# Layer 0's softmax weights in four buffers instead of three, with one buffer less for the sums of key tiles, the denominator and the numerator

## The chip, the cores and the metric

The kernel runs on one core of a Trainium2 chip. The metric is the device time of the whole program in microseconds. The core has five engines that run side by side and meet through semaphores: TensorE (PE, whose weight loads are listed apart as PEld), VectorE (DVE), ScalarE (ACT), GpSimd (POOL) and SyncE (SP, which issues the DMAs here). Everything is computed in fp32.

## The reference

Two attention layers on an image `x` of 128 rows by 256 places by 256 channels, each with a group norm ahead of it and a residual around it. The change lies in the first one, layer 0, with 8 heads of 32 channels:

```python
def _L0_conv_ref(msa_repr, pair_repr, gate_proj, qkv_proj, out_proj, bias_proj):
    bias = jnp.einsum('nijz,zh->nhij', pair_repr, bias_proj)[:, None]
    gate = jax.nn.sigmoid(msa_repr @ gate_proj).reshape(bs, s, r, head, c)
    q, k, v = jnp.split(msa_repr @ qkv_proj, 3, axis=-1)
    ...
    sim = jnp.einsum('nsqhc,nskhc->nshqk', q, k) * scale
    sim = jax.nn.softmax(sim, axis=-1)
    sim = sim + bias
    attend = jnp.einsum('nshqk,nskhc->nsqhc', sim, v) * gate
    out = attend.reshape(bs, s, r, cm) @ out_proj
    return out

x = x + _L0_conv_ref(_gn(x), ...)     # layer 0
x = x + _L1_conv_ref(_gn(x), ...)     # layer 1: 4 heads of 64 channels, a band of 16 places
```

The softmax runs over 256 keys for each of 256 queries, separately in each of the 128 rows and 8 heads. Since the bias is added after the softmax, the kernel computes `((sum of e v) / z + (sum of bias v)) * gate`, where `e` are the exponentials and `z` their sum.

## The kernel before, in words

The program has three stretches. The first one loads `x` for the statistics and turns the pair bias into `bias_sb`. The second one, the loop of layer 0, takes the 128 image rows one by one. The third one does the same for layer 1. Layer 0 writes its rows to a buffer in DRAM, from which layer 1 reads.

In the loop of layer 0, channels or keys lie on the 128 partitions. The 256 keys make two key tiles (`kt`), and the 8 heads make two halves of four heads (`half`). For a row `s`, the functions do this:

- `scores(s, half)`: 8 products `sim` on PE (line 640), four heads side by side in strips of 32 partitions, into four PSUM banks, one for each head. Then four exponentials `ex` on ACT (line 651), one for each bank. A buffer of `ex` holds four heads by two key tiles by 256 queries, 8 KB in a partition, so a row fills two of them.
- `join_tiles(s, half, j)`: DVE adds the two key tiles of two heads into `both` (line 657), 4 KB in a partition, two instructions for a half.
- `sum_heads(s)`: PE multiplies `both` by ones, so that `zs` (line 681) is the softmax denominator, and multiplies the bias by `v`, which gives `bv` (line 667).
- `divide(s, zs)`: ACT copies `zs` to `z` (line 694). DVE makes the denominator `d` with the gate (line 696) and its reciprocal (line 697).
- `attend(s)`: PE multiplies `ex` by `v`, which gives `av` (line 667, 32 records for a row, the first half of the heads before the second). DVE makes the numerator `t` as `bv * z + av` (lines 712 and 713) and `at` as `t * d` (line 715).
- `stretch(names, i)`: the projections of the pair of rows `i`, `q` and `k` in one step of the loop, `v` and `g` (the gate) in the next, with PE and ACT taking turns: `f.take("15")` and its like are copies on ACT (lines 621 to 627), and `p2qk` or `p2vg` collect one product of each.
- `by_channel(out_sb, ...)` gives `po` on PE (line 513), and `finish` adds the residual on DVE (line 723).

The loop works one row behind itself: step `s` computes the scores of row `s` and finishes row `s - 1`. The order on PE, ACT and DVE is the order in which the program text issues the instructions (`manual_schedule`); only POOL's instructions are placed by a scheduler. One step issues:

```python
scores(s, 0); zs = sum_heads(s - 1); join_tiles(s, 0, 0); divide(s - 1, zs)
# in even steps: ACT makes the exponential of g (line 786)
scores(s, 1); attend(s - 1)
join_tiles for (0, 2), (1, 0), (1, 2); least(s - 1, z)
stretch(...); normal(s + 4); finish(s - 1, by_channel(out_sb, ...))
```

The score tiles and the projections share a ring of five PSUM banks, taken in turn; a step takes 12 tiles from it (8 scores, 3 in `stretch`, 1 for `po`). `av`, `bv` and `zs` have one bank each.

Each tile tag of a pool has a number of buffers (`bufs`), used in turn. The pool `att0` holds `ex`, `both`, `z`, `d` and `t`, with two buffers for each tag that doesn't say otherwise. Before, `ex` and `both` have three. The first instruction that writes a buffer anew waits until the last reader of its former content has ended. With three buffers of `ex`, the second half of row `s` takes the buffer of the first half of row `s - 1`, which `attend(s - 1)` reads. With three buffers of `both`, the first half of row `s` takes that of the second half of row `s - 2`.

Of the kernel before, what the change touches and what calls it, by code (L numbers as in the profile page):

```python
# [9 lines left out]
F32 = mybir.dt.float32  # L10
# [5 lines left out]
P = 128  # L16
R = 256
# [22 lines left out]
def conv_preact_kernel(  # L40
# [38 lines left out]
    def sim_bank(name):  # L79
        return bank("sim", name)  # L80
# [45 lines left out]
    for part, first in ((seen[:, 0], 0), (seen_high, -KB)):  # L126
        nc.gpsimd.memset(part, 1.0)
        for b in range(NB):
            d = first + KB * b - QLO[b]
# [409 lines left out]
    with ExitStack() as both:  # L539
# [11 lines left out]
        with ExitStack() as lay0:  # L551
            row = lay0.enter_context(tc.tile_pool(name="row0", bufs=2))
            att = lay0.enter_context(tc.tile_pool(name="att0", bufs=2))
# [79 lines left out]
            def scores(s, half):  # L633
                i, r = divmod(s, 2)
                q, k = res["q", i], res["k", i]
                sims = [sim_bank(f"sim{s}_{half}_{j}") for j in range(4)]
                for kt in range(2):
                    for j in range(4):
                        p0 = D0 * j
                        nc.tensor.matmul(  # L640
                            sims[j][:, kt, :],
                            lhsT=k[p0 : p0 + D0, 2 * r + half, kt * P : (kt + 1) * P],
                            rhs=q[p0 : p0 + D0, 2 * r + half, :],
                            start=True, stop=True,
                        )
                ex = att.tile([P, 4, 2, R], F32, tag="ex", name=f"ex{s}_{half}", bufs=3)
                both = att.tile([P, 4, R], F32, tag="both", name=f"both{s}_{half}", bufs=3)
                hd[s, half] = (ex, both)

                for j in range(4):  # L650
                    nc.scalar.activation(ex[:, j], sims[j], AF.Exp, scale=1.0 / math.sqrt(D0))  # L651
# [7 lines left out]
            def products(to, s, weights):  # L659

                i, r = divmod(s, 2)
                v = res["v", i]
                for half in range(2):
                    for kt in range(2):
                        for j in range(4):
                            c0 = kt * P + j * D0
                            nc.tensor.matmul(  # L667
                                to[D0 * j : D0 * (j + 1), half, :],
                                lhsT=v[:, 2 * r + half, c0 : c0 + D0], rhs=weights(4 * half + j, kt),
                                start=(kt == 0), stop=(kt == 1),  # L670
                            )
# [17 lines left out]
            def divide(s, zs):  # L689
                if s < 0:  # L690
                    return
                i, r = divmod(s, 2)
                z = att.tile([P, 2, R], F32, tag="z", name=f"z{s}")
                nc.scalar.activation(z, zs, AF.Identity, accum_out=zsum[:, s : s + 1])
                d = att.tile([P, 2, R], F32, tag="d", name=f"d{s}")
                nc.vector.scalar_tensor_tensor(d, res["g", i][:, 2 * r : 2 * r + 2, :], 1.0, z, op0=ALU.add, op1=ALU.mult)
                nc.vector.reciprocal(d, d)  # L697
                hd[s, "z"] = (z, d)
# [5 lines left out]
            def attend(s):  # L704
                if s < 0:
                    return
                (ex0, _), (ex1, _), bv0 = hd.pop((s, 0)), hd.pop((s, 1)), hd.pop(s)
                av = ps_av.tile([P, 2, R], F32, tag="av", name=f"av{s}")
                products(av, s, lambda h, kt: (ex0, ex1)[h // 4][:, h % 4, kt, :])
                z, d = hd.pop((s, "z"))  # L710
                t = att.tile([P, 2, R], F32, tag="t", name=f"t{s}")
                nc.vector.tensor_tensor(t, bv0, z, ALU.mult)
                nc.vector.tensor_tensor(t, av, t, ALU.add)
                at = row.tile([P, 2, R], F32, tag="at", name=f"at{s}")
                nc.vector.tensor_tensor(at, t, d, ALU.mult)  # L715
                st[s]["at"] = at
# [52 lines left out]
            with tc.manual_schedule(engines={mybir.EngineType.PE, mybir.EngineType.Activation, mybir.EngineType.DVE}):  # L769
# [8 lines left out]
                for s in range(S + 1):  # L778
                    if s < S:
                        scores(s, 0)  # L780
                    zs = sum_heads(s - 1)
                    join_tiles(s, 0, 0)
                    divide(s - 1, zs)
                    if s % 2 == 0 and s < S:
                        e = res["g", s // 2]
                        nc.scalar.activation(e, e, AF.Exp, scale=-1.0)
                    if s < S:
                        scores(s, 1)
                    z = hd[s - 1, "z"][0] if s > 0 else None
                    attend(s - 1)  # L790
                    for half, j in ((0, 2), (1, 0), (1, 2)):
                        join_tiles(s, half, j)
                    least(s - 1, z)
                    if s == S - 1:
                        most1 = join_most(st1, stats1, 1)
                        load1(0)
                        load1(1)
                    stretch(("qk", "vg")[s % 2], s // 2 + 1)
                    normal(s + 4)
                    if s % 2 == 1:  # L800
                        sum_rows((s + 3) // 2)
                    if s > 0:
                        finish(s - 1, by_channel(out_sb, 0, st[s - 1]["at"], f"po{s - 1}"))
# [6 lines left out]
        with ExitStack() as lay:  # L810
            ps_av = psum(lay, "1", 4, 0)
            row = lay.enter_context(tc.tile_pool(name="row1", bufs=4))
            att = lay.enter_context(tc.tile_pool(name="att1", bufs=2))
# [146 lines left out]
            for s in range(0, S + 4, 2):  # L960
                pair = lambda first: (first, first + 1)
                if s < S:
                    for r in pair(s):
                        scores(r)
                if s <= S:
                    for r in pair(s - 2):
                        attend(r)
                for r in pair(s - 4):
                    project(r)
                for r in pair(s + 2):  # L970
                    for n in (1, 2):
                        piece(r, n)
                for r in pair(s + 2):
                    piece(r, 3)
                for r in pair(s + 4):
                    piece(r, 0)
                for r in pair(s - 4):
                    finish(r)
                if s <= S:
                    for r in pair(s - 2):  # L980
                        divide(r)
# [195 lines left out]
```

## Time and profile before

| what | value |
|---|---|
| time, median of 3 runs (lowest to highest) | 3416.61 us (3416.49 to 3417.72) |
| profiled execution: time, span of its instructions | 3416.59 us, 3414.9 us |
| PE busy | 3303.8 us, 97% |
| DVE, ACT, POOL busy | 2560.7, 1768.3, 1139.6 us |
| loop of layer 0, about 337 to 2245 us | 1908 us, PE busy 1864 us |
| one step of that loop, mean of two | 15.77 us |
| reciprocal of `d`, one | 3353 ns |
| exponential `ex`, one | 603 ns |
| mean granted TensorE clock | 0.988 |

The profile is of one execution. Busy time is the time in which an engine had an instruction under way; the profiler models the ends of matmuls, so a busy PE can still have slack in the distance between the starts of two matmuls. The steps of layer 0 come in two kinds: with `q` and `k` in their `stretch`, and with `v` and `g`. A row's products on PE come as merged pieces in the timeline: `x32` is 32 matmul records in one piece.

### The profile page before, as it was taken

What the parts mean: (1) busy time and instruction counts of PE and PEld (TensorE: products, weight loads), DVE (VectorE), ACT (ScalarE), POOL (GpSimd) and SP (SyncE); (2) the same over time, 40 slices, a digit from 0 to 9 for tenths busy, and PEclk for the clock granted to TensorE, in tenths of its full rate; (3) what the DMA queues carried; (4) which work ended last, traced back from release to release, by engine and by line L of the source; (5) the groups of instructions that cost most, each with busy time, mean ns of one, the idle gap of its engine ahead of it and who ended that gap; (6) DMA issues with size and microseconds to landing.
All of it is one profiled execution on the core that took longest, in us unless ns stands there. A gap on an engine that the chain in (4) does not pass through costs nothing.

```text
span 3414.9 us, 86753 instructions
## 1 busy us (share of the span) xinstructions
PE 3303.8 (97%) x37193; PEld 2488.6 (73%) x37193; DVE 2560.7 (75%) x3794; ACT 1768.3 (52%) x3866; POOL 1139.6 (33%) x1135
## 2 busy tenths in 40 slices
PE   6899999999999999999999999989999999999997
PEld 4566666666666666666666666678888888888886
DVE  4747877777787787777778777757777777777776
ACT  4565555555555555555555555534444444444442
POOL 3033333333333333333333333223333333333332
PEclk8999999999999999999999999999999999999999
DMA  9922111111111111111111111002222222222221
GB/s 380 409 58 57 44 36 35 35 35 32 38 32 32 38 32 38 32 38 32 32 38 32 37 33 32 20 20 64 53 62 63 64 61 54 63 64 63 55 60 45
DMA packets 346328, 209.37 MB, mean 61 GB/s; under 512 B 273608, under 2 KB 339152, under 8 KB 339664
## 3 DMA queue, kind: packets, MB, share of 16 engines
q1 hardware_dynamic: 345040, 201.37, 20.4%
q8 instruction: 295, 4.83, 0.6%
q0 software_dynamic: 752, 2.36, 0.2%
q14 instruction: 97, 0.79, 0.1%
q10 hardware_dynamic: 144, 0.00, 0.0%
HBM read 136.59 MB, written 67.11 MB: 60 GB/s over the span
## 4 chain that ended last, share of the span: by engine, by line
PE 87%; ACT 5%; DMA 3%; DVE 3%; issue 1%; SPq 0%; ACTq 0%; POOL 0%; DVEq 0%
PE sim L640 8%; PE p1v L841 7%; PE av L667 7%; PE 1po L513 7%; PE p1q L513 7%; PE po L513 7%; PE p1k L513 6%; PE bv L667 6%; PE pv L614 6%; PE pq L610 5%; PE pk L610 4%; PE zs L681 4%; DMA xs<-in_x_dram 3%; PE pg L610 3%; PE 1sim L862 3%; PE 1avz L894 2%
## 5 line engine op out<-in xcount | busy, mean ns | idle before, releaser
L651 ACT ACTIVATE ex<-sim 128x512 f32<-128x512 f32 x1024 | 528.6, 603 | 500.4 <-PE sim L640 274.8
L919 DVE RECIPROCAL 1rz<-1z 128x512 f32<-128x512 f32 x128 | 427.9, 3343 | 174.2 <-ACT 1z L917 174.2
L872 POOL TENSOR_TENSOR 1p<-1ex,seen 128x768 f32<-128x768 f32 x128 | 233.8, 1826 | 735.9 <-ACT 1ex L870 735.9
L657 DVE TENSOR_TENSOR both<-ex 128x512 f32<-128x512 f32 x512 | 340.9, 707 | 125.0 <-ACT ex L651 124.9
L697 DVE RECIPROCAL d<-d 128x512 f32<-128x512 f32 x128 | 429.2, 3353 | 4.4
L640 PE MATMUL sim<-q,k 32*128 32x256 f32 x4096 | 295.9, 401 | 1.1 <-ACT ex L651 1.1
L630 POOL TENSOR_TENSOR v<-v,twovg 128x256 f32<-128x256 f32 x64 | 46.5, 726 | 736.1 <-ACT twovg L756 736.1
L833 ACT ACTIVATE 1q<-p1q,bqk 128x256 f32<-128x256 f32 x256 | 107.3, 470 | 345.0 <-PE p1q L513 345.0
L640 PEld LDWEIGHTS sim<-q,k 32*128 32x128 f32 x4096 | 187.0, 184 | 102.3 <-issue 88.0
L513 PE MATMUL po<-at,out_sb 128*128 128x256 f32 x1024 | 247.2, 385 | 11.8 <-DVE at L715 11.8
L667 PE MATMUL av<-ex,v 128*32 128x256 f32 x4096 | 247.5, 382 | 0.0
L513 PE MATMUL 1po<-1at,w_out_t 128*128 128x256 f32 x1024 | 242.0, 390 | 5.0 <-DVE 1at L921 5.0
L513 PE MATMUL p1q<-xn,w_in_t 128*128 128x256 f32 x1024 | 243.8, 381 | 2.0 <-DVE xn L493 1.1
L667 PE MATMUL bv<-bias_sb,v 128*32 128x256 f32 x4096 | 244.5, 379 | 0.0
L513 PE MATMUL p1k<-xn,w_in_t 128*128 128x256 f32 x1024 | 241.9, 379 | 0.0
L841 PE MATMUL p1v<-w_in_t,xn 128*64 128x128 f32 x4096 | 237.9, 274 | 0.0
L841 PEld LDWEIGHTS p1v<-w_in_t,xn 128*64 128x64 f32 x4096 | 222.3, 137 | 21.5 <-issue 21.5
L513 PEld LDWEIGHTS 1po<-1at,w_out_t 128*128 128x128 f32 x1024 | 191.3, 192 | 54.8 <-ACT 1z L917 23.9
L723 DVE TENSOR_TENSOR o<-po,xt 128x512 f32<-128x512 f32 x128 | 88.6, 692 | 190.0 <-PE po L513 190.0
L513 PEld LDWEIGHTS po<-at,out_sb 128*128 128x128 f32 x1024 | 197.8, 194 | 40.4 <-issue 7.7
L630 POOL TENSOR_TENSOR q<-q,twoqk 128x256 f32<-128x256 f32 x64 | 46.5, 727 | 529.3 <-ACT twoqk L756 529.3
L513 PEld LDWEIGHTS p1q<-xn,w_in_t 128*128 128x128 f32 x1024 | 195.6, 191 | 29.2 <-issue 1.3
(226 smaller groups left out, 6748.1 us busy)
## 6 DMA issues: line engine op xcount, KB each, us to landing
pr<-in_L_conv_pair_repr_dram SPq DMA_DIRECT2D x32, 1024.0 KB, 23.3
x<-o SPq DMA_DIRECT2D x64, 512.0 KB, 2.8
yg<-x SPq DMA_DIRECT2D x64, 512.0 KB, 4.3
out_dram<-1o SPq DMA_DIRECT2D x256, 128.0 KB, 4.1
xg<-in_x_dram SPq DMA_DIRECT2D x252, 128.0 KB, 3.2
xs<-in_x_dram SPq DMA_DIRECT2D x15, 2048.0 KB, 21.7
xs<-in_x_dram SPq DMA_DIRECT2D x2, 1024.0 KB, 17.9
qkv_sb<-in_L_conv_qkv_proj_dram POOLq DMA_DIRECT2D x4, 192.0 KB, 13.4
```

The lines of the kernel that those rows point to most:

```text
L513: nc.tensor.matmul(ps[:, m, :], lhsT=w[:, kt, col + m * P : col + (m + 1) * P], rhs=xn[:, kt, :], start=(kt == 0), stop=(kt == 1),)
L610: nc.tensor.matmul(out, lhsT=stationary(self.w, n), rhs=moving, start=first, **flags)
L614: nc.tensor.matmul(out[:, cols], lhsT=moving[:, cols], rhs=stationary(self.w, n), start=first and t2 == 0, **flags)
L640: nc.tensor.matmul(sims[j][:, kt, :], lhsT=k[p0 : p0 + D0, 2 * r + half, kt * P : (kt + 1) * P], rhs=q[p0 : p0 + D0, 2 * r + half, :], sta ...
L651: nc.scalar.activation(ex[:, j], sims[j], AF.Exp, scale=1.0 / math.sqrt(D0))
L657: nc.vector.tensor_tensor(both[:, j : j + 2], ex[:, j : j + 2, 0, :], ex[:, j : j + 2, 1, :], ALU.add)
L667: nc.tensor.matmul(to[D0 * j : D0 * (j + 1), half, :], lhsT=v[:, 2 * r + half, c0 : c0 + D0], rhs=weights(4 * half + j, kt), start=(kt == ...
L681: nc.tensor.matmul(zs[D0 * j : D0 * (j + 1), half, :], lhsT=ones[:, 0:D0], rhs=both[:, j, :], start=True, stop=True,)
L697: nc.vector.reciprocal(d, d)
L841: nc.tensor.matmul(ps[KB * half : KB * (half + 1), b, :], lhsT=xn[:, kt, KB * b : KB * (b + 1)], rhs=w_in_t[:, kt, 2 * C + P * half : 2 * ...
L872: nc.gpsimd.tensor_tensor(p.rearrange("p j (r c) -> p (j r) c", c=WROW)[:, :, 0 : 2 * WSTEP] .rearrange("p r (t c) -> p r t c", c=WSTEP)[: ...
L919: nc.vector.reciprocal(rz, z)
```

## The change

`ex` gets a fourth buffer. Each half of row `s` then takes the buffer of the same half of row `s - 2`, which `attend(s - 2)` read in the step before. `both` goes from three buffers to two, so the first half of row `s` takes that of the first half of row `s - 1`, which the `zs` products of the same step read. `d` and `t` go from two buffers to one. In a partition, `ex` takes 8 KB more, `both` 4 KB less, `d` and `t` 2 KB less each, so the pool's size stays as it was. The order of the instructions on every engine stays as it was too; what differs is which semaphores some of them wait for.

```diff
-                ex = att.tile([P, 4, 2, R], F32, tag="ex", name=f"ex{s}_{half}", bufs=3)
-                both = att.tile([P, 4, R], F32, tag="both", name=f"both{s}_{half}", bufs=3)
+                ex = att.tile([P, 4, 2, R], F32, tag="ex", name=f"ex{s}_{half}", bufs=4)
+                both = att.tile([P, 4, R], F32, tag="both", name=f"both{s}_{half}")
...
-                d = att.tile([P, 2, R], F32, tag="d", name=f"d{s}")
+                d = att.tile([P, 2, R], F32, tag="d", name=f"d{s}", bufs=1)
...
-                t = att.tile([P, 2, R], F32, tag="t", name=f"t{s}")
+                t = att.tile([P, 2, R], F32, tag="t", name=f"t{s}", bufs=1)
```

In the built programs these waits differ, step by step: the first exponential of a second half no longer waits for DVE, and its wait for PE now means its own score tile; each of the other three gets a wait for its own tile, which the first one's later wait had covered. The first `both` of a row gets a wait for PE. The first product of `p2qk` or `p2vg` loses a wait for PE and keeps that for ACT. The copy of `g` gets a wait for DVE.

## The prediction

> **What bounds the kernel now.** I read the page first. PE (TensorE) is busy for 97% of the span and holds 87% of the chain that ended last; ACT holds 5%, DVE 3%. The loop of layer 0, where all four edits lie, runs from about 337 to 2245 us: 1908 us, with PE busy 1864 us. The page also shows what the fourth buffer aims at: the exponentials have 500 us of idle time before them.
>
> ```profile
> PE 3303.8 (97%) x37193; PEld 2488.6 (73%) x37193; DVE 2560.7 (75%) x3794; ACT 1768.3 (52%) x3866; POOL 1139.6 (33%) x1135
> PE 87%; ACT 5%; DMA 3%; DVE 3%; issue 1%; SPq 0%; ACTq 0%; POOL 0%; DVEq 0%
> L651 ACT ACTIVATE ex<-sim 128x512 f32<-128x512 f32 x1024 | 528.6, 603 | 500.4 <-PE sim L640 274.8
> ```
>
> Idle time on ACT costs only what PE later waits for. So I asked next who waits for whom, PE and its weight loads (PEld) alone, from 400 to 2150 us (111 rows of 15.77 us). A line gives engine, line, releaser, total us, times, longest.
>
> ```profile
> PE pq L610 <- ACT midq L625: 8.8, 56, 0.2
> PE pv L614 <- ACT midv L623: 0.4, 1, 0.4
> ...
> PEld sim L640 <- issue: 77.5, 210, 0.4
> ...
> PEld pq L610 <- ACT ex L651: 23.1, 56, 0.4
> PEld pv L614 <- ACT ex L651: 22.6, 55, 0.4
> ```
>
> PE waits for ACT's small copies, never for `ex`. Two rows of PEld do name `ex`, 45.7 us in all: either a real stall or only a neighbour in time. Last, the timeline of one row from 1313 us: ACT alone, DVE alone, and the PE pieces between. Columns: start, duration, engine, line, operation; in brackets the idle time before it and what ended it.
>
> ```profile
> 1315.34 2.06 ACT L651 ACTIVATE ex<-sim 128x512 f32<-128x512 f32 x4 [2.14 <-PE sim L640]
> ...
> 1317.83 1.09 ACT L786 ACTIVATE g<-g 128x1024 f32<-128x1024 f32 x1
> 1320.19 2.06 ACT L651 ACTIVATE ex<-sim 128x512 f32<-128x512 f32 x4 [1.27 <-PE av L667]
> 1322.11 0.62 ACT L621 COPY q<-pq 128x512 f32<-128x512 f32 x1
> 1322.95 0.59 ACT L621 COPY k<-pk 128x512 f32<-128x512 f32 x1 [0.21 <-PE pk L610]
> ```
>
> ```profile
> 1315.25 1.07 PE L681 MATMUL zs<-both,ones 128*32 128x256 f32 x16
> ...
> 1317.97 0.74 PEld L640 LDWEIGHTS sim<-q,k 32*128 32x128 f32 x16 [0.41 <-issue]
> ...
> 1319.05 1.93 PE L667 MATMUL av<-ex,v 128*32 128x256 f32 x32
> ...
> 1320.91 0.30 PEld L610 LDWEIGHTS pq<-xn,qkv_sb 128*128 128x128 f32 x2 [0.41 <-ACT ex L651]
> ```
>
> ```profile
> 1316.45 0.69 DVE L657 TENSOR_TENSOR both<-ex 128x512 f32<-128x512 f32 x1 [1.48 <-ACT ex L651]
> 1318.07 0.90 DVE L696 SCALAR_TENSOR_TENSOR d<-g,z 128x512 f32<-128x512 f32 x1 [0.93 <-ACT z L694]
> ...
> 1323.73 0.69 DVE L715 TENSOR_TENSOR at<-t,d 128x512 f32<-128x512 f32 x1
> 1324.34 1.89 DVE L657 TENSOR_TENSOR both<-ex 128x512 f32<-128x512 f32 x3
> ```
>
> The wait is plain: the second half's exponentials start at 1320.19, 1.27 us after ACT went idle, because their buffer is still read by the first half of `av`. The trap is the 0.41 us before `pq`. The switch from `bv` to `sim` at 1317.97 has the same 0.41 and no ACT in it. In the records, start of the last `av` matmul to start of the first `pq` or `pv` is 309 ns in all 111 rows; `bv` to `sim` is 309 ns in all 111, `po` to `sim` too. A switch that is equally long where ACT plays no part isn't waiting for ACT.
>
> **What the Trainium skill says.** "TensorEngine Tiling (Array Packing)", Key Properties: changing the tiling mode drains TensorE. The trace agrees: PEld pauses 0.33 to 0.41 us wherever the tile shape changes (`sim` 32*128, `zs` 128*32, `pq` 128*128), and not between `zs` and `bv`, which share one. "Perfetto Trace Analysis", Optimization Strategy: the same gap repeated on the engine that should be saturated can mean too few buffers. Here the repeated gap is on ACT, 52% busy, so the sentence doesn't make it worth time. Same page, Identifying Dependency Chains: an instruction waiting on several engines may get an EventSemaphore ahead of it. The trace has them: 222 on ACT at L651 in those 111 rows, and on PE at 51 ns each.
>
> **The change part by part.**
>
> *ex, three to four buffers.* Removed: the wait of the second half's exponentials for `av`. They can start once their `sim` is there. The first half shows the lag: `sim` at 1314.17, `ex` at 1315.34, so 1.17 us. The second half's `sim` starts at 1317.97, so `ex` at about 1319.14 instead of 1320.19: 1.05 us earlier (ACT is free at 1318.92, after the exponential of `g`). The other kind of row, with `pv` and `pg`, goes from 1304.40 to 1302.14 + 1.17 = 1303.31: 1.09 us. Over 127 rows ACT gains some 136 us of lead. Who uses it? (a) PE needs the banks that the exponentials free. The five banks go round, 12 tiles a row: `pq` takes the bank of the first half's last score tile, `pk` that of `ex` number 1 of the second half (free at 1320.79, used at 1321.88), `p2qk` that of number 2 (free near 1321.27, used at 1322.75). None is late. (b) The next copy on ACT, `q` at 1322.11, has its product at 1322.05, so it can come 0.01 us earlier; `v` in the other row is 0.04 us late at most. PE writes that bank again at 1323.61, 0.88 us after the copy ends. From the `k` copy on, ACT waits for PE, so the lead is gone. (c) DVE adds the second half's key tiles at 1324.34, behind `at`, when `ex` has been done for 2 us. Path: 0. From below, were all 309 - 216 = 93 ns of that switch a wait: 127 x 93 ns = 11.8 us gained. I take 0.
>
> *both, three to two.* Added: the first key-tile sum of a row waits for the `zs` products of the row before. All 16 end at 1316.32 and the sum starts at 1316.45, held by `ex`; the eight it needs end 0.4 us sooner. Behind it on DVE stands `d`, with 0.93 us of idle time, then the reciprocal, `t`, `at`, for which `po` waits. To cost anything the sum must slip over 0.93 us. 0, and nothing from above: its releaser has ended before the wait begins. A gain has no way in.
>
> *d and t, two to one.* Writer and last reader are both DVE, in order: `at` of one row (to 1324.42) comes before the next row's `d` (some 10 us on). 0; what hides it is DVE's own other work.
>
> *Small waits.* The `p2` product loses its second wait, the first sum gains one, `g`'s copy gains one on DVE. At PE's 51 ns an extra semaphore instruction is worth 127 x 51 ns = 6.5 us if bare. But `p2qk` follows the product before it after 216 ns, a plain slot; DVE idles 0.16 to 1.48 us before the sum; ACT idles 0.20 us before `g`'s copy. I take 0, from -6.5 to +6.5 us. No DMA and no work on SP or POOL moves.
>
> *Neighbours.* The exponentials now run beside all of `av`, not its last half. In the records groups of four `av` matmuls start 216 ns apart before and after `ex` starts, and `bv` runs beside the first half's exponentials at the same 216. 0.
>
> Sum: 0 against the profiled execution (3414.9 us of span, 3416.59 in all), which stands 0.02 us under the median of 3416.61. What remains is the clock: the pauses at the end of layer 0 are followed by stretches of 3.4 us at a granted 0.50 in the windows view, and one such stretch more or less is 1.7 us of work. Two either way make 3.4.
>
> **The rivals.** *Faster.* ACT's lead is used after all: the row "PEld pq <- ACT ex" is a real wait. For: the profile names it. Against: the twin switch of 309 ns. Price: 11.8 us, so 3404.8 us. Chance 0.05.
>
> *Slower.* Exponentials beside the first half of `av` slow its matmuls, since ACT writes one `ex` buffer while PE streams another. Place: the first four of eight groups; price: per ns and group 4 x 127 = 0.5 us. It decides (over 0.2%, 6.8 us) from 13 ns a group, 6%. At 10% of 216 ns it is 11 us: 3427.6 us. For: this overlap is new for those groups. Against: the last four groups already run so, at 216 ns. "PSUM — Partial Sum Buffer", PSUM bank collisions, says that a clash in a bank raises an error, not a stall; no run here shows it. Chance 0.07.
>
> *It doesn't do what it says.* Something else holds the exponentials, such as `g`'s, which ends just 0.2 us before they could start. Then nothing moves: same time, inside the likeliest case.
>
> **How the numbers follow.** No change: 0.88, at 3416.6 us. A measurement of this kernel tells about 0.2% from no change, 6.8 us. Within 3.5 us either way comes the clock's spread; I widen to 3412.6 and 3420.6 for about half of the bare semaphore bound. That leaves out both rivals, 0.12, and a little of the main case.
>
> **What would show it.** Right: the row "ACT ex <- PE av" is gone, the second half's `ex` starts about 1.05 us sooner against `sim`, new idle time of about 1 us stands before the copies of `q` and `v`, the PEld switch into `pq` is still 0.41 us, and `zs`, `d` and `po` keep their distances, the row its 15.77 us. Wrong: a switch into `pq` below 309 ns (faster), or `av` groups over 216 ns or `d` later against `zs` (slower).

## The result, and the profile after

The changed kernel takes 3417.65 us (median of 4 runs, 3411.70 to 3418.18) beside 3416.94 us for the kernel before (4 runs): a ratio of 0.9998 over all these runs, not of the two medians, with a 95% interval of 0.9981 to 1.0015. The forecast of no change, at 3416.6 us, holds.

The wait that the fourth buffer was to remove is gone all the same. This is the page's group of exponentials in the profile after; its last columns are the idle time before them and what ended most of it. The idle time was 500.4 us before.

```profile
L651 ACT ACTIVATE ex<-sim 128x512 f32<-128x512 f32 x1024 | 528.8, 603 | 362.9 <-PE sim L640 362.9
```

So 137.5 us of ACT's idle time left that place. Where did it go? This is the timeline of one row of the profile after, ACT alone, from 1310 us on. It answers to the ACT lines of the prediction.

```profile
1310.95 2.07 ACT L651 ACTIVATE ex<-sim 128x512 f32<-128x512 f32 x4 [2.14 <-PE sim L640]
...
1313.45 1.09 ACT L786 ACTIVATE g<-g 128x1024 f32<-128x1024 f32 x1
1314.75 2.07 ACT L651 ACTIVATE ex<-sim 128x512 f32<-128x512 f32 x4 [0.22 <-PE sim L640]
1317.70 0.59 ACT L621 COPY q<-pq 128x512 f32<-128x512 f32 x1 [0.88 <-PE pq L610]
1318.56 0.59 ACT L621 COPY k<-pk 128x512 f32<-128x512 f32 x1 [0.28 <-PE pk L610]
```

The second half's exponentials now wait 0.22 us instead of 1.27, and for their own scores. The copy of `q`, which had no idle time before it, now has 0.88 us, released by PE. ACT moved its pause from ahead of the exponentials to behind them. The same row on the other engines, taken from timelines of the profile after:

```profile
1310.86 1.07 PE L681 MATMUL zs<-both,ones 128*32 128x256 f32 x16
...
1313.59 0.74 PEld L640 LDWEIGHTS sim<-q,k 32*128 32x128 f32 x16 [0.41 <-issue]
...
1314.67 1.93 PE L667 MATMUL av<-ex,v 128*32 128x256 f32 x32
...
1316.53 0.30 PEld L610 LDWEIGHTS pq<-xn,qkv_sb 128*128 128x128 f32 x2 [0.41 <-ACT ex L651]
```

```profile
1312.07 0.69 DVE L657 TENSOR_TENSOR both<-ex 128x512 f32<-128x512 f32 x1 [1.48 <-ACT ex L651]
1313.69 0.90 DVE L696 SCALAR_TENSOR_TENSOR d<-g,z 128x512 f32<-128x512 f32 x1 [0.93 <-ACT z L694]
...
1319.35 0.69 DVE L715 TENSOR_TENSOR at<-t,d 128x512 f32<-128x512 f32 x1
1319.96 1.89 DVE L657 TENSOR_TENSOR both<-ex 128x512 f32<-128x512 f32 x3
```

Measured from the start of `sim` (1313.59 here, 1317.97 before), `ex` starts after 1.16 us instead of 2.22, and `pq` after 2.94 us as before. On DVE every bracket is the one of before. So PE and DVE did the same things at the same distances.

The records say it more finely. From one row's first `zs` matmul to the next row's is 15.774 us in the mean (rows 3 to 124), 15.771 before: 0.003 us a row, 0.4 us over the loop. The medians of the two kinds of rows, 15.835 and 15.701 us before, are the same within 0.001 us. The profiled spans differ by more, 3410.0 against 3414.9 us, and that difference isn't the change's: the first `zs` comes at 222.5 us instead of 226.9, ahead of the first buffer that is used anew. The windows view shows the granted clock there (window, length, busy PE, PEld, DVE, ACT, POOL, the granted clock, then DMA); first before, then after.

```profile
0.00:220.00 220.00, 173.75 (x1075) 118.63 (x1076) 125.17 (x595) 119.88 (x244) 41.44 (x123) 0.89 0.86 326
```

```profile
0.00:220.00 220.00, 168.05 (x1089) 112.10 (x1089) 125.22 (x595) 120.47 (x249) 41.77 (x124) 0.95 0.86 326
```

The granted clock was 0.89 in one execution and 0.95 in the other. Of the 4.4 us, 3.0 arise between the first `sim` (at 210.2 us before, 208.9 after) and the first `zs`. There the profile before has a stretch at half the clock and the profile after has none; the same two matmuls of `pq`, before and after, show what that costs:

```profile
213.90:220.80 6.90, 6.90 (x23) 5.09 (x23) 4.34 (x8) 4.51 (x8) 2.78 (x3) 0.51 0.00 0
```

```profile
215.91 1.22 PE L610 MATMUL pq<-xn,qkv_sb 128*128 128x256 f32 x2
```

```profile
213.60 0.70 PE L610 MATMUL pq<-xn,qkv_sb 128*128 128x256 f32 x2
```

For the other 1.4 us, which lie ahead of the first `sim`, the lower clock is the likely cause and not a shown one.

### The profile page after: what moved, and what is told of

Same layout as the page of the kernel before. It is cut to its first block, busy times and chain, and to the rows that moved or that the text cites. A ratio compares the mean times of both kernels' runs of the same rounds, so it can differ in the third digit from the quotient of the medians.

```text
span 3410.0 us, 86688 instructions
## 1 busy us (share of the span) xinstructions
PE 3292.2 (97%) x37193; PEld 2476.5 (73%) x37193; DVE 2554.7 (75%) x3794; ACT 1781.7 (52%) x3866; POOL 1140.2 (33%) x1135
## 4 chain that ended last, share of the span: by engine, by line
PE 87%; ACT 5%; DMA 3%; DVE 3%; issue 1%; SPq 0%; ACTq 0%; POOL 0%; DVEq 0%
PE sim L640 8%; PE p1v L841 7%; PE av L667 7%; PE 1po L513 7%; PE p1q L513 7%; PE p1k L513 7%; PE po L513 6%; PE bv L667 6%; PE pv L614 6%; PE pq L610 5%; PE pk L610 4%; PE zs L681 4%; DMA xs<-in_x_dram 3%; PE pg L610 3%; PE 1sim L862 3%; PE 1avz L894 2%
## 5 line engine op out<-in xcount | busy, mean ns | idle before, releaser
L657 DVE TENSOR_TENSOR both<-ex 128x512 f32<-128x512 f32 x512 | 332.8, 690 | 121.4 <-ACT ex L651 121.3
```

The lines of the kernel that those rows point to most:

```text
L657: nc.vector.tensor_tensor(both[:, j : j + 2], ex[:, j : j + 2, 0, :], ex[:, j : j + 2, 1, :], ALU.add)
```

## The experiments

The theory: PE's own order and its waits for ACT's small copies set the time of a row. Three buffers of `ex` make the exponentials late, but not so late that anything on PE waits. The rivals: a gain of `ex` is paid back by `both`; or ACT's lead is lost again at once.

### The other three buffers alone

```diff
-                ex = att.tile([P, 4, 2, R], F32, tag="ex", name=f"ex{s}_{half}", bufs=4)
+                ex = att.tile([P, 4, 2, R], F32, tag="ex", name=f"ex{s}_{half}", bufs=3)
```

(against the kernel after.)

> The buffers of both, d and t as after, ex still three. Theory of the prediction (each part costs nothing by itself): 3417 us, within 0.2% of before, the first both of a row still starts 0.16 or 1.48 us after DVE went idle and is released by ex, d still 0.93 us after. Rival (a gain of the fourth ex buffer is paid back by the wait of both for zs): slower than before by what the buffer gains, at least 7 us, 3424 us or more, with both released by PE zs.

Measured: 3417.08 us (13 runs), ratio to before 1.0001, interval 0.9993 to 1.0009; 15.772 us a row. The waits of DVE from 400 to 2050 us (what waited, on whom, us, times, longest) show who releases the first sum:

```profile
DVE d L696 <- ACT z L694: 90.4, 104, 0.9
DVE both L657 <- ACT ex L651: 86.8, 105, 1.5
```

All 105 are released by `ex`, none by `zs`. There is no price, so there is nothing for a gain to be hidden behind: both are zero, as far as rows that agree within 0.003 us can tell.

### More work on ACT, with three and with four buffers

If the lead is real but idle, it must become worth time once ACT has more to do. A copy of weights onto themselves, right behind the second half's exponentials, uses it up:

```diff
                     if s < S:
                         scores(s, 1)
+                        nc.scalar.copy(w_in_t, w_in_t)
```

> Before, plus one copy of 1536 elements a partition (the weights w_in_t onto themselves) on ACT in each step, right after the second half's exponentials; some 1.45 us of ACT, an estimate from 603 ns for 512 and 1087 ns for 1024 elements. Theory: with three buffers PE has 0.80 us of slack against the copies of q, k, v and g that follow; 0.65 us a row is lost, 127 rows, 83 us: about 3500 us. Rival (ACT's place after the exponentials has no bearing on PE at all): 3417 us.

> After, plus the same copy of 1536 elements. Theory: the fourth buffer gives ACT 1.05 us of lead, slack 1.85 us, more than 1.45 us: nothing lost, 3417 us, some 83 us less than the same load with three buffers. Rival (the lead is lost somewhere else, the exponentials being held by something behind the wait that was removed): as with three buffers, about 3500 us.

Measured: with three buffers 3501.97 us (4 runs), ratio 1.025, interval 1.0234 to 1.0265. With four, 3416.13 us (12 runs), ratio 1.0000, interval 0.9991 to 1.0008. First ACT's timeline with three buffers, then with four:

```profile
1301.23 2.06 ACT L651 ACTIVATE ex<-sim 128x512 f32<-128x512 f32 x4 [1.27 <-PE av L667]
1303.16 1.49 ACT L789 COPY w_in_t<-w_in_t 128x1536 f32<-128x1536 f32 x1
1304.52 0.62 ACT L621 COPY q<-pq 128x512 f32<-128x512 f32 x1
```

```profile
1319.46 2.06 ACT L651 ACTIVATE ex<-sim 128x512 f32<-128x512 f32 x4 [0.22 <-PE sim L640]
1321.38 1.50 ACT L789 COPY w_in_t<-w_in_t 128x1536 f32<-128x1536 f32 x1
1322.74 0.62 ACT L621 COPY q<-pq 128x512 f32<-128x512 f32 x1
```

And PE's waits from 400 to 2050 us with three buffers, which the kernel before doesn't have:

```profile
PE pq L610 <- ACT q L621: 23.2, 50, 0.5
PE pv L614 <- ACT v L621: 19.6, 51, 0.7
```

With three buffers the copy of `q` comes so late that the next `pq` product waits for it; a row takes 16.449 us, 0.678 more. With four, PE has no wait for these two copies left, and a row takes 15.770 us. The same edit of the buffers that was worth nothing is worth 86 us here. The lead of 1.05 us is real; the kernel just has no use for it.

### A shorter load on ACT, with three buffers

```diff
                     if s < S:
                         scores(s, 1)
+                        nc.scalar.copy(w_in_t[:, 0, 0:512], w_in_t[:, 0, 0:512])
```

> Before, plus a copy of 512 elements of w_in_t onto themselves at the same place, some 0.5 us of ACT. Theory: under the slack of 0.80 us of three buffers, so no change, 3417 us. Rival (PE already waits for ACT at the switch from av to pq or pv, so any delay of ACT is paid in full): 0.5 us a row, 3480 us.

Measured: 3415.93 us (12 runs), ratio 1.0000, interval 0.9991 to 1.0008; 15.773 us a row. The copies of `q` and `v` end 0.51 us later than before, and that costs nothing. So the rival, that any delay of ACT at this place is paid in full, is out. Whether PE waits for `ex` itself this run can't tell, since the added copy stands behind the exponentials.

### What does set the time of a row

If PE's waits for the small copies are what counts, filling them must pay, with three buffers as with four. The four products of `po` were taken from behind `stretch` and put into it, one at a time. The edit is shortened here; `parts` issues one product whenever it is asked for the next:

```diff
                 f.take("6")
+                next(parts, None)          # one product of po
                 f.product(3)
...
                 f.product(7)
+                next(parts, None)
                 g.product(7)
                 f.take("7")
                 g.take("7")
+                next(parts, None)
                 f.product(4)
...
                 g.take("34")
+                for part in parts: pass    # the last one
```

> After, with the four po products of the row before put one by one into the places of stretch where PE waits for a copy of ACT (ahead of product 3 of the first name, ahead of product 7 of the second, ahead of product 4 of the first, the last one at the end). Theory (PE's own order and its waits for the small copies set the time of a row, the exponentials don't): the starts of the matmuls there lose 193 + 193 + 321 = 0.71 us a step against their 216 ns, a po product fills 432 ns; 125 steps, 88 us less: about 3328 us. Rival (at is ready too late for the first place, only 0.2 us ahead of it, and po now stalls): half of it or less, 3370 us or more.

> Before, with the same placing of po. Theory: the products that the copies after the exponentials must precede (product 6) stand ahead of the moved ones, so their 0.80 us of slack stays and three buffers do as well as four: about 3328 us, within 0.2% of the same with four. Rival (in a shorter step the exponentials of three buffers come too late and the fourth buffer pays): slower than with four by 0.2% or more.

Measured: with four buffers 3335.08 us (4 runs), ratio 0.9768, interval 0.9750 to 0.9785; with three 3332.45 us (4 runs), ratio 0.9764, interval 0.9746 to 0.9781. A row takes 15.118 and 15.113 us. The kernel before took 3413.84 us beside them (6 runs). Both are 2.3% faster than it, and the number of `ex` buffers makes no difference here either: 0.005 us a row in the mean and 0.001 us in the medians of the two kinds of rows. The 2.6 us between the times are more than the 0.6 us that the mean makes, and lie inside both intervals.

The saving is 0.655 us a row, not 0.71. Two terms of the expectation were off against each other. The stalls themselves are gone, and they were 0.71 us. But after each of them the second matmul had also started late, by 75 to 104 ns, so the three cost 0.30 us more than was counted. And a new wait of 0.35 us came behind, among the first `sim` of the next row: 0.71 + 0.30 - 0.35 = 0.66. PE's timeline of the run with four buffers, which read `1.15` for `sim` in that place before:

```profile
1313.54 0.59 PE L814 MATMUL po<-at,out_sb 128*128 128x256 f32 x2
1314.06 1.50 PE L640 MATMUL sim<-q,k 32*128 32x256 f32 x16
```

Of the four heads side by side, three start in time and the fourth is 0.37 us late. Its weight load waits for a semaphore of ACT and starts 51 ns after the last copy of `stretch` (line 627) has ended, in all 112 rows between 400 and 2100 us. That copy empties one of the five banks that the scores take in turn. The whole of `po` used to stand between (1.73 us); now one product does (0.43 us). No run took this wait away.

## Why the prediction was right

*The lead.* Forecast: `ex` 1.05 us earlier, from a lag of 1.17 us. Measured: 1.06 us earlier, lag 1.16. Forecast: new idle time of about 1 us ahead of the copy of `q`; measured 0.88. Forecast: no use for it; the row's 15.771 us became 15.774. Since the exponentials now wait for their own scores, the rival that something else holds them is out too.

*The trap at the switch.* The prediction read 0.41 us with `ex` named as releaser as the price of the change of tile shape, on the strength of a twin. The profile after settles it: `ex` starts 1.06 us sooner against PE, and PEld still shows the same totals, still with the same name. Waits of PEld from 400 to 2150 us, after:

```profile
PEld pq L610 <- ACT ex L651: 23.1, 56, 0.4
PEld pv L614 <- ACT ex L651: 22.6, 55, 0.4
```

Start to start it is 309 ns in all 111 rows, as it was. The exponential that ends last ahead of `pq` or `pv` ends 0.08 to 0.13 us ahead of the first matmul of the new shape in the profile before and 0.20 us ahead of it in the profile after (rows between 400 and 2100 us). A wait for it could not have kept the same 309 ns in both. So the faster rival is out.

*The wait of both.* It was to lie behind `ex`. In the profile after and in the run with the three smaller edits alone the brackets are unchanged, with `ex` as the releaser. A wait for `zs` shows once, 1.8 us in one row of the run with `po` moved and four buffers.

*d, t and the small waits.* Nothing was seen of them: the run without the fourth buffer has the row of before within 0.001 us. What the removal of PE's second wait at `p2qk` does by itself was not tried apart; with all the edits that product still starts 216 ns after the one before it.

*Neighbours.* `av`'s groups start 216 ns apart in the median and 219.3 ns in the mean, before and after. The slower rival is out.

*The clock and the range.* The clock term was right in kind, and at the end of layer 0 in size: there the profile before has one stretch of 3.4 us at half the clock more, and the last step of the loop but one, from `zs` to `zs`, takes 13.72 us instead of 12.09. But the larger difference between the two profiles lies ahead of the loop, where the prediction didn't look. And the range is narrow. The working widens the 3.5 us of the clock to 4.0 for about half of the bare semaphore bound, but half of 6.5 us is 3.25. Of the 33 runs of the kernel before that stand beside the experiments, 8 lie under 3412.6 us; of the changed kernel's 4 runs, the profiled one does, at 3411.70. The medians lie inside, those of the kernel before too (3413.84 to 3416.94). So the range fits a median and not a single execution.

Two other numbers need a word, and neither carried the forecast. The loop of layer 0 begins at 210 us, with the first `sim`, and not at 337: the prediction and the table quote a window that cuts off its first 127 us. The slack of the copies, 0.80 us in the expectations, comes out of the run with the long copy: the copies behind it ended 1.36 us later, and the product that waits for them started 0.63 us late in rows with `q` and `k`, 0.54 us in rows with `v` and `g`. That leaves 0.73 and 0.82 us of slack. The row grew by more, 0.678 us, because the second matmul after the new stall is late as well. That 0.65 us was expected there is in part luck: the copy was to delay ACT by 1.45 us, and the late second matmul wasn't counted.

## What to carry to other kernels

A wait that a buffer causes is worth what its victims on the bounding engine wait for, so follow the late instruction to the next one that PE needs, and count the slack there before counting the idle time. A releaser that the profile names can be a neighbour in time: look for a twin of the gap where the named engine has no part. And to see whether a lead is real, load the engine that has it, with and without the change.

## What the runs showed of the hardware

- At a switch between tile shapes the first matmul starts 304 to 309 ns after the last one of the old shape (`bv` to `sim`, `po` to `sim`, `av` to `pq`: 309; `sim` to `zs`, `sim` to `av`: 304), in every run. From `zs` to `bv`, which share a shape, it is 196 ns.
- After a pause the second matmul is late too. Where PE had stalled for a copy of ACT, the second matmul of `pq` starts 320 or 291 ns after the first instead of 216. The same 320 ns stand behind the switches into `sim` (where four heads count as one) and `pq`. So such a pause costs up to 104 ns more than the gap that shows it.
- A row of the loop repeats within a few nanoseconds across executions (15.770 to 15.774 us in five kernels with the same PE order), while whole executions of one kernel spread over 8 us (3410.48 to 3418.72 in 33 runs). For a change inside a loop, the distance between equal instructions in the trace tells far finer than the time.
